# Adding two planes to loaded sums inside the transfer: the dense stage of a convolution-attention hybrid with mixture of experts

## The chip, the cores and the metric

The kernel runs on one core of a Trainium2 chip. The metric is device time in microseconds of one execution. A core has TensorE (PE, matrix products), VectorE (DVE), ScalarE (ACT), GpSimd (POOL) and SyncE (SP); SP, ACT and POOL issue transfers, which sixteen DMA engines carry out. "PEld" in a profile is PE's weight loads. Matrix products go to PSUM, from where VectorE and ScalarE read them.

## What is computed

The input is eight images of 256 channels by 32 x 32, seen as eight items of 1024 tokens with 256 numbers each, all in f32. Cut to what matters:

```python
x = _L0_conv_ref(x, w_qkv, b_qkv, w_out, b_out)   # attention, 8 heads, plus x
t = _to_tokens(x)
t = t + _L1_attn_ref(_ln_t(t), W)                 # attention of tokens on themselves
t = t + _L1_ffn_ref(_ln_t(t), router_w, w1, b1, w2, b2)
x = _from_tokens(t, x)

def _moe(tokens, router_w, w1, b1, w2, b2):       # inside _L1_ffn_ref, 8 experts, top 2
    probs = softmax(tokens @ router_w.T)
    rw, re = top_k(probs, 2);  rw = rw / rw.sum(-1)
    out = tokens
    for e in range(8):
        h = gelu(tokens @ w1[e] + b1[e])
        out = out + combine[:, e:e+1] * (h @ w2[e] + b2[e])
    return out
```

`combine` holds a token's two weights `rw` at its two experts and zero at the other six.

## The kernel before

The items go through the layers one after the other, b = 0 to 7. Items 0 to 6 ("the others") are routed: after their second norm, `dispatch` scatters each token's normed row, twice (once for each of its two experts), into a DRAM tensor of rows sorted by expert. Their running sums (tokens after attention plus the normed tokens) are kept in DRAM as `sums[b]`, 128 partitions x 8 blocks x 256. While item 7 goes through its attention, `experts` works off the 63 blocks of the others' rows, and GpSimd scatters each block's scaled results by an indirect transfer (L1466) into the DRAM tensor `y`. `y` is laid out as two planes: plane k holds, for every token of the others, what its k-th expert gave. `planes[n]` is the view of item n's two planes with the same shape as `sums[n]`. So an other item's final value is `sums[n] + planes[n][0] + planes[n][1]`.

Item 7 itself is not routed. `dense` (L1588) runs all eight experts over all its tokens. Its loop goes over e = 0 to 7 and the two halves n of the tokens, 16 steps. In each step `hidden` makes the first product (`pdh`, L1630, eight PE instructions in the profile) and the gelu on ScalarE (L1639), and `collect` the second product of the step before (`pdy`, L1654, sixteen instructions), which VectorE multiplies by the gate and adds into `t2` (L1664, four instructions of 128 x 256). `pdy` goes to the PSUM pool `ps_acc`, which has two buffers; each holds half of a step's result, so PE can go on with `pdy` only as VectorE's adds free a buffer. `biases` (after the third `hidden`) uses the same two buffers for `pb` (L1618), which VectorE adds into `t2` (L1621).

The class `Results` finishes the others in the shadow of this loop. It has 14 pieces of work, the halves of seven items, each 128 x 1024 f32 = 512 KB. Up to five are in flight. For each one SP loads the half of `sums` into a `total` tile (L1539) and the halves of both planes into a slot (L1541). `collect` calls `others.tick` once a step, after the step's last gated add: `add` puts two VectorE adds of 128 x 1024 behind it (L1551), and `store` transposes the total in 32 x 32 squares (L1573, VectorE) and sends four transfers of 128 KB to the output (L1579); then SP's next loads for that tile are issued. From the step after that on, the gated adds are issued behind the transposition (`others.last`). The last step stores item 7's own second half in two parts, and its transfers alternate between SP and ACT. The transposed tiles `oT` have two buffers.

Each engine's instructions run in the order in which they stand in its queue. Where a transfer has to wait for a landing or for an instruction, its issuing queue waits, and all behind it.

Before the loop, GpSimd's queue ends with the last block's two indirect transfers and four tensor adds (L1120), which put the normed tokens onto item 7's sum.

Of the kernel before, what the change touches and what calls it, by code (L numbers as in the profile page):

```python
# [10 lines left out]
F32 = mybir.dt.float32  # L11
I32 = mybir.dt.int32
AF = mybir.ActivationFunctionType
ALU = mybir.AluOpType
# [5 lines left out]
def kernel(  # L20
# [23 lines left out]
    nc = tc.nc  # L44
    P = 128
    B, C, S = x.shape
    E, D, FF = w1.shape
# [22 lines left out]
    one = ctx.enter_context(tc.tile_pool(name="one", bufs=1))  # L70
    two = ctx.enter_context(tc.tile_pool(name="two", bufs=2))
# [8 lines left out]
    NEXP = 6  # L80
    exp_turn = [0]

    def exp_tile(name, at=None):
        if at is None:
            at = exp_turn[0] % NEXP
            exp_turn[0] += 1
        return expp.tile([P, 1024], F32, tag=f"exps{at}", name=name)
# [148 lines left out]
    NB = NT // NH2  # L236
# [5 lines left out]
    class Split:  # L242

        def __init__(self, first, last):
            self.first, self.last = first, last
# [477 lines left out]
    def attend(b, t1, fill, tick=nothing, n1=None):  # L723
# [28 lines left out]
        for ec in range(NCC):  # L752
            px = big(f"px_{b}_{ec}")
            for dc in range(NCC):
                for n in range(NH2):
                    nc.tensor.matmul(  # L756
                        px[:, ts(n, 512)],
                        WT[:, dc, ts(ec, P)],
                        nT[:, dc, ts(n, 512)],
                        start=(dc == 0),  # L760
                        stop=(dc == NCC - 1),
                    )
            pxs.append(px)
            if ec == 0:
                nc.scalar.copy(a11, px[:, :HALF])
                tick(("xa", ec), nc.vector.tensor_sub(s3_, a11, px[:, HALF:]))
            else:
                nc.scalar.copy(a12, px[:, :HALF])
                nc.scalar.copy(a22, px[:, HALF:])
                nc.vector.tensor_add(s1_, a22, pxs[0][:, HALF:])  # L770
                nc.vector.tensor_sub(s2_, s1_, a11)
                tick(("xa", ec), nc.vector.tensor_sub(s4_, a12, s2_))
# [5 lines left out]
        class Pair:  # L778
# [61 lines left out]
            def rest(self, behind=None):  # L840
# [9 lines left out]
                def even():  # L850
                    tick(("max", 2 * k), self.add(ex0[:, HALF:], self.z, self.low[0], nmax[0]))
                    if k != 1:
                        self.soften()
# [243 lines left out]
    def normed(b, t2, fill, tick=nothing, norm=None):  # L1097

        if norm is None:
            n2 = one.tile([P, NT, DW], F32, tag="n", name=f"n2_{b}")  # L1100
            tokens = n2[:, :, :D]
            tick("normed", layer_norm(t2, tokens, 1e-5, f"f{b}"))
        else:
            n2 = tokens = norm.dst
            written = norm.blocks(NT - 1, NT)
            tick("normed", written)
        fill("norm 2")
        nT = one.tile([P, NCC, S], F32, tag="nT", name=f"n2T_{b}")
        copied = to_channels(tokens, nT, f"n2_{b}")
        tick("turned", copied)  # L1110

        if norm is None:
            nc.gpsimd.tensor_add(t2, t2, tokens)
        else:
            with tc.issue_after(copied.ins):
                fill("turned")
            for part, at in ((n2.first, slice(0, NT - 1)), (n2.last, slice(NT - 1, NT))):
                for cc in range(NCC):
                    some = t2[:, at].rearrange("p i (k cc c) -> p cc i k c", k=NQ, c=SQ)[:, cc]
                    added = nc.gpsimd.tensor_add(  # L1120
                        some, some, part[:, :, ts(cc, P)].rearrange("p i (k c) -> p i k c", c=SQ)
                    )
                    tc.add_manual_dep(added.ins, evicted["scaled"].ins.name, BEHIND)
        fill("normed 2")
        l = logits(b, nT, rT if norm is None else rTs)
        return n2, nT, l
# [191 lines left out]
    def experts(group, behind, table, steps):  # L1318
# [109 lines left out]
        def collect(b, hT, last, squares):  # L1428
            wb, rs = seconds.pop(b), group.size[b] // P
            py = acc(f"pe_{n}_{b}")  # L1430
            at = NCC * FF
            with tc.issue_after(last.ins) if last else nullcontext():
                for r in range(rs):
                    for fc in range(NFC):
                        mm = nc.tensor.matmul(  # L1435
                            py[:, ts(r, D)],
                            hT[:, fc, ts(r, P)],
                            wb[:, ts(fc, D)],
                            start=(fc == 0),
                            stop=(fc == NFC - 1),  # L1440
                        )
            yb = two.tile([P, rs, D], F32, tag="yb", name=f"yb_{n}_{b}")

            def add():
                return nc.vector.tensor_add(
                    yb,
                    py[:, : rs * D].rearrange("p (r d) -> p r d", d=D),
                    b2_flat[:, bass.ds(register(b, 3), D)].unsqueeze(1).to_broadcast([P, rs, D]),
                )

            if squares is not None:
                with tc.issue_after(squares.ins):
                    add()
                    send(b, yb)
            return mm, add, yb
# [45 lines left out]
        def result(b, whole=True):  # L1501
            mm, add, yb = collect(b, hiddens.pop(b), None, None)
            if whole:
                add()
                return send(b, yb)
            return add, lambda: send(b, yb)
# [3 lines left out]
    class Results:  # L1510


        def __init__(self, group):
            self.group = group
            self.todo = [(n, h) for n in range(len(group.items)) for h in range(NH2)]
            wide = one.tile([P, 2, 2, NB, D], F32, tag="v", name="ys_v")
            self.slots = [
                two.tile([P, 2, NB, D], F32, tag="xT", name="ys_0"),
                wide[:, 0],
                two.tile([P, 2, NB, D], F32, tag="xT", name="ys_3"),  # L1520
                wide[:, 1],
                one.tile([P, 2, NB, D], F32, tag="n", name="ys_4"),
            ]
            self.totals = [
                exp_tile(f"total_{i}", i).rearrange("p (i d) -> p i d", d=D)
                for i in range(len(self.slots))
            ]
            self.sent, self.added, self.stored = 0, 0, 0
            self.last = None
            for _ in self.slots:  # L1530
                self.load()

        def load(self):
            if self.sent == len(self.todo):
                return
            n, h = self.todo[self.sent]
            at = self.sent % len(self.slots)
            self.sent += 1
            nc.sync.dma_start(self.totals[at], self.group.sums[n][:, ts(h, NB), :])  # L1539
            for k in range(2):  # L1540
                nc.sync.dma_start(  # L1541
                    self.slots[at][:, k], self.group.planes[n][:, k, ts(h, NB), :]
                )

        def add(self, behind):
            at = self.added % len(self.slots)
            self.added += 1
            total = self.totals[at]
            with tc.issue_after(behind.ins):
                for k in range(2):  # L1550
                    added = nc.vector.tensor_add(total, total, self.slots[at][:, k])  # L1551
            return added

        def store(self, behind):
            at = self.stored % len(self.slots)
            n, h = self.todo[self.stored]
            self.stored += 1
            with tc.issue_after(behind.ins):
                self.last = store(self.group.items[n], self.totals[at], h)
            self.load()  # L1560

        def tick(self, behind):
            if self.added < len(self.todo):
                self.store(self.add(behind))

    def store(b, total, n, parts=1):

# [20 lines left out]
    def dense(b, t2, norm, fill, begin, table):  # L1588
# [59 lines left out]
        def collect(e, n, hT, behind):  # L1648
# [29 lines left out]
            if (e, n) == (E - 1, 0):  # L1678
                with tc.issue_after(added.ins):
                    others.last = store(b, t2[:, ts(n, NB), :], n)  # L1680
# [18 lines left out]
    for b in range(B):  # L1699
        xT = next_x  # L1700
# [7 lines left out]
        if b + 1 < B:  # L1708
            begun = Begin(b + 1, next_x)
            t2 = attend(b, t1, begun.at)  # L1710
            n2, _, l = normed(b, t2, begun.at)
# [85 lines left out]
```

## Time and profile before

| what | us |
|---|---|
| median of three runs (2268.3 to 2272.7) | 2271.99 |
| the profiled execution's own time | 2274.83 |
| its span, first to last instruction | 2273.1 |
| PE busy over the span | 2231.4 (98%) |
| VectorE busy | 1567.1 (69%) |
| GpSimd busy | 309.7 (14%) |
| first product of the dense loop (`pdh`) | starts 2144.28 |
| first pair of plane adds | starts 2158.58 |
| first plane load issued by SP | 2150.06 |
| last transposition | 2267.98, 0.71 long |

How to read it: the profile is one execution, with times counted from the span's start. Its windows give the busy time of each engine in a stretch, with the clock that TensorE was granted (1.00 is full speed) and the mean busy share of the 16 DMA engines; that share can read a little over 1. A timeline row gives start, duration, engine, line, operation, output and inputs and how often it stands there in a row; in brackets is how long the engine sat idle before it and who released it. In the dense loop, a plane load of 512 KB landed a median of 6.4 to 8.1 us after its issue, the load of a total 4.7 us after, a store of 128 KB 3.8 us.

### The profile page before, as it was taken

The numbers are of one execution on the slowest core, as the hardware profiler recorded it, in microseconds if no ns is written. First come the engines' busy times: TensorE is split into PE (matmuls) and PEld (weight loads), VectorE is DVE, ScalarE is ACT, GpSimd is POOL, SyncE is SP. The second block draws the span as 40 slices with busy tenths as digits, with TensorE's granted clock in tenths as the row PEclk, the third lists the DMA queues.
The fourth block names the chain that finished last, engine by engine and source line by source line (L and its number), as shares of the span: only waits on it lengthen the run. The fifth ranks groups of instructions, "written<-read, shape, count | busy, mean of one in ns | idle before, by whom it ended". The sixth has DMA issues, their size and how long they took to land.

```text
span 2273.1 us, 38013 instructions
## 1 busy us (share of the span) xinstructions
PE 2231.4 (98%) x13033; PEld 1200.3 (53%) x13033; DVE 1567.1 (69%) x3924; ACT 1231.3 (54%) x2221; POOL 309.7 (14%) x327
## 2 busy tenths in 40 slices
PE   9999999999999999999999999999999999999998
PEld 3345534563356335543555345534563368885666
DVE  5775678567865787577756775678557857665667
ACT  3664566356636564746554664566355655555411
POOL 1000012000300030002000120002000315551100
PEclk9999999999999999999999999999999999999999
DMA  8996201020102010111011010200032036662485
GB/s 279 357 352 199 53 15 43 3 61 7 51 1 46 19 51 7 31 35 43 15 19 46 20 38 10 55 13 27 1 78 64 31 70 148 149 148 48 120 276 169
DMA packets 273449, 181.89 MB, mean 80 GB/s; under 512 B 191860, under 2 KB 228519, under 8 KB 272232
## 3 DMA queue, kind: packets, MB, share of 16 engines
q1 hardware_dynamic: 260328, 149.16, 24.3%
q0 software_dynamic: 11296, 29.78, 3.6%
q8 instruction: 104, 1.70, 0.3%
q14 instruction: 89, 0.73, 0.1%
q10 hardware_dynamic: 1632, 0.52, 0.1%
HBM read 62.55 MB, written 105.70 MB: 74 GB/s over the span
## 4 chain that ended last, share of the span: by engine, by line
PE 80%; issue 5%; ACT 4%; DVE 4%; SPq 2%; POOL 2%; DMA 1%; POOLq 0%; DVEq 0%; ACTq 0%
PE po L608 20%; PE psc L531 20%; PE pqk L384 7%; PE py L925 7%; PE pr L716 5%; PE pv L414 4%; PE ps L819 3%; PE px L756 2%; POOL y L1466 2%; SPq L908 2%; PE pdh L1630 2%; PE pdy L1654 2%; PE pqk L362 2%; PE ps1z L819 2%; PE ph L1406 1%
## 5 line engine op out<-in xcount | busy, mean ns | idle before, releaser
L572 ACT ACTIVATE ex<-psc,nmax 128x1024 f32<-128x1024 f32 x512 | 570.4, 1115 | 298.8 <-DVE scrap L555 215.6
L608 PE MATMUL po<-ex,vs 64*64 64x512 f32 x4096 | 568.5, 592 | 5.3 <-DVE vs L588 4.3
L531 PE MATMUL psc<-qk,qk 64*64 64x512 f32 x4096 | 566.0, 593 | 3.7 <-ACT ex L572 3.6
L555 DVE TENSOR_SCALAR_CACHE_REDUCE scrap<-psc,nmax 128x512 f32<-128x512 f32 x512 | 384.5, 751 | 158.5 <-PE psc L531 129.8
L546 DVE TENSOR_REDUCE nmax<-psc 128x1 f32<-128x512 f32 x512 | 350.8, 685 | 10.7 <-PE psc L531 10.7
L531 PEld LDWEIGHTS psc<-qk,qk 64*64 64x64 f32 x4096 | 178.0, 132 | 275.1 <-ACT ex L572 129.0
L608 PEld LDWEIGHTS po<-ex,vs 64*64 64x64 f32 x4096 | 172.9, 132 | 284.0 <-DVE vs L588 87.6
L1203 POOL DMA_INDIRECT rows<-n,d_at x112 | 109.2, 975 | 463.4 <-DVE nmax L546 425.1
L384 PE MATMUL pqk<-xT,wqkv 128*128 128x512 f32 x384 | 171.2, 599 | 0.0
L1466 POOL DMA_INDIRECT y<-yb,to x119 | 117.4, 986 | 209.2 <-DVE yb L1459 185.6
L349 ACT ACTIVATE qk<-pqk,b_qks 128x512 f32<-128x512 f32 x124 | 85.6, 690 | 88.8 <-PE pqk L384 79.7
L384 PEld LDWEIGHTS pqk<-xT,wqkv 128*128 128x128 f32 x384 | 71.0, 190 | 99.9 <-issue 77.3
L908 ACT COPY spare<-home 32x256 f32<-32x256 f32 x272 | 109.4, 402 | 17.3 <-DVE home L896 11.9
L414 PE MATMUL pv<-wqkv,xT 128*128 128x512 f32 x244 | 116.4, 600 | 1.0 <-DVE v L436 1.0
L925 PE MATMUL py<-n,spare 128*128 128x256 f32 x512 | 114.9, 379 | 0.0
L1195 POOL IOTA n<- 128x8 f32 x14 | 2.0, 145 | 820.5 <-PE py L925 820.5
L1406 PE MATMUL ph<-xb,w_ring 128*128 128x256 f32 (+1 forms) x488 | 110.7, 370 | 2.9 <-DVE xb L1395 2.8
L716 PE MATMUL pr<-wo,res 128*128 128x256 f32 x512 | 111.9, 379 | 0.7 <-ACT res L627 0.7
L925 PEld LDWEIGHTS py<-n,spare 128*128 128x128 f32 x512 | 96.4, 190 | 20.1 <-issue 4.3
L716 PEld LDWEIGHTS pr<-wo,res 128*128 128x128 f32 x512 | 97.2, 190 | 17.8 <-ACT res L627 4.7
L1418 ACT ACTIVATE hb<-ph,b1T 128x256 f32<-128x256 f32 (+1 forms) x126 | 51.3, 459 | 101.1 <-PE ph L1406 101.1
L1435 PE MATMUL pe<-w_ring,hb 128*128 128x256 f32 x444 | 105.5, 379 | 0.0
(265 smaller groups left out, 2836.8 us busy)
## 6 DMA issues: line engine op xcount, KB each, us to landing
rows<-zero SPq DMA_DIRECT2D x7, 8256.0 KB, 62.4
xr<-rows SPq DMA_DIRECT2D x224, 64.0 KB, 2.0
xs<-in_x_dram SPq DMA_DIRECT2D x64, 128.0 KB, 3.9
ys<-y SPq DMA_DIRECT2D x16, 512.0 KB, 6.4
spare<-home SPq DMA_DIRECT2D x240, 32.0 KB, 1.9
out_dram<-oT SPq DMA_DIRECT2D x58, 128.0 KB, 3.8
xT<-in_x_dram SPq DMA_DIRECT2D x7, 1024.0 KB
sums<-t SPq DMA_DIRECT2D x7, 1024.0 KB
```

The costliest lines, as they stand in the source:

```text
L384: mm = nc.tensor.matmul(pq[:, ts(n, 512)], wqkv[:, cc, t, ts(g, P)], xT[:, cc, ts(n, 512)], start=(cc == 0), stop=(cc == NCC - 1),)
L414: return nc.tensor.matmul(pv, self.xT[:, cc, ts(i, P)], wqkv[:, cc, 2, :], start=(cc == 0), stop=(cc == NCC - 1),)
L531: mm = nc.tensor.matmul(pss[at, h][ts(c, DK), ts(n, 512)], k[r, j * P + c * DK : j * P + (c + 1) * DK], q[r, ts(n, 512)], start=True, stop ...
L546: firsts[at, h] = nc.vector.tensor_reduce(nmax, pss[at, h][:, ts(0, 512)], AX.X, ALU.max, negate=True)
L555: seconds[h] = nc.vector.tensor_scalar(scrap, pss[at, h][:, ts(1, 512)], -1.0, nmaxes[at, h], ALU.mult, ALU.min, accum_out=nmax,)
L572: nc.scalar.activation(ex, pss.pop((at, h)), AF.Exp, bias=nmaxes.pop((at, h)), scale=1.0, accum_out=sums[at][:, h : h + 1],)
L608: mm = nc.tensor.matmul(po[n][ts(h, DK), :], vss[at][keys, h, :], exps[at, h][keys, ts(n, 512)], start=(j == 0 and turn == 0), stop=(j == ...
L716: nc.tensor.matmul(pr[:, :C], res[g][:, ts(i, P)], wo[:, g, :], start=(g == 0), stop=(g == NPAIR - 1))
L908: move(to[ts(k, SQ), a], since[ts(a, SQ), k])
L925: evicted["mixed"] = nc.tensor.matmul(py[:, :D], aT[m], n1[:, m, :], start=(m == 0), stop=(m == NT - 1))
L1406: last = nc.tensor.matmul(ph[:, ts(fc, br)], wb[:, dc * FF + fc * P : dc * FF + (fc + 1) * P], xb[:, dc, :], start=(dc == 0), stop=(dc == ...
L1466: sent = nc.gpsimd.indirect_dma_start(out=group.ways[sum(group.size[:b]) // P + r][:, :], out_offset=bass.IndirectOffsetOnAxis(ap=to[:, r ...
```

## The change

The two planes are no longer loaded into slots of their own. GpSimd issues, for each plane, a transfer that adds what it reads to the `total` tile it writes. The VectorE adds and the slots go; the number of totals in flight is six (`NEXP`) in place of five. SP still loads the totals, and the transposition and the stores stay as they are. In the order in which GpSimd's queue is built, plane 0 of the first three totals comes first, then plane 1 of these three, then the same for the next three; from the seventh total on, plane 0 and plane 1 of a total follow each other. They stand behind the four adds of L1120. The second accumulation into a total waits for the first to have landed, and the first for the load of the sum.

```diff
         def __init__(self, group):
             self.group = group
             self.todo = [(n, h) for n in range(len(group.items)) for h in range(NH2)]
-            wide = one.tile([P, 2, 2, NB, D], F32, tag="v", name="ys_v")
-            self.slots = [
-                two.tile([P, 2, NB, D], F32, tag="xT", name="ys_0"),
-                wide[:, 0],
-                two.tile([P, 2, NB, D], F32, tag="xT", name="ys_3"),
-                wide[:, 1],
-                one.tile([P, 2, NB, D], F32, tag="n", name="ys_4"),
-            ]
             self.totals = [
-                exp_tile(f"total_{i}", i).rearrange("p (i d) -> p i d", d=D)
-                for i in range(len(self.slots))
+                exp_tile(f"total_{i}", i).rearrange("p (i d) -> p i d", d=D) for i in range(NEXP)
             ]
...
         def load(self):
...
-            at = self.sent % len(self.slots)
+            total = self.totals[self.sent % len(self.totals)]
             self.sent += 1
-            nc.sync.dma_start(self.totals[at], self.group.sums[n][:, ts(h, NB), :])
+            nc.sync.dma_start(total, self.group.sums[n][:, ts(h, NB), :])
             for k in range(2):
-                nc.sync.dma_start(
-                    self.slots[at][:, k], self.group.planes[n][:, k, ts(h, NB), :]
-                )
-
-        def add(self, behind):
-            at = self.added % len(self.slots)
-            self.added += 1
-            total = self.totals[at]
-            with tc.issue_after(behind.ins):
-                for k in range(2):
-                    added = nc.vector.tensor_add(total, total, self.slots[at][:, k])
-            return added
+                nc.gpsimd.dma_start(
+                    total, self.group.planes[n][:, k, ts(h, NB), :], accum_op=ALU.add
+                )
...
         def tick(self, behind):
-            if self.added < len(self.todo):
-                self.store(self.add(behind))
+            if self.stored < len(self.todo):
+                self.store(behind)
```

More of the change, by code (lines that the diff above doesn't have):

```diff
@@ L1529, in __init__ @@
             self.last = None
-            for _ in self.slots:
+            for _ in self.totals:
                 self.load()
@@ L1536, in load @@
             n, h = self.todo[self.sent]
-            at = self.sent % len(self.slots)
+            total = self.totals[self.sent % len(self.totals)]
             self.sent += 1
-            nc.sync.dma_start(self.totals[at], self.group.sums[n][:, ts(h, NB), :])
+            nc.sync.dma_start(total, self.group.sums[n][:, ts(h, NB), :])
             for k in range(2):
-                nc.sync.dma_start(
-                    self.slots[at][:, k], self.group.planes[n][:, k, ts(h, NB), :]
-                )
-        def add(self, behind):
-            at = self.added % len(self.slots)
-            self.added += 1
-            total = self.totals[at]
-            with tc.issue_after(behind.ins):
-                for k in range(2):
-                    added = nc.vector.tensor_add(total, total, self.slots[at][:, k])
-            return added
+                nc.gpsimd.dma_start(
+                    total, self.group.planes[n][:, k, ts(h, NB), :], accum_op=ALU.add
+                )
         def store(self, behind):
-            at = self.stored % len(self.slots)
+            at = self.stored % len(self.totals)
             n, h = self.todo[self.stored]
```

## The prediction

> **What bounds the kernel now.** I read the windows of the last 130 us first, then the engines' timelines there, then the chain of waits. The page says PE 98% busy overall, so the question is whether the dense stage (from about 2147 us on) is PE's too, and how much room its other resources have. The windows (busy time of PE, PEld, DVE, ACT, POOL; then granted clock, DMA share, GB/s):
>
> ```profile
> 2156.00:2159.00 3.00, 3.00 (x8) 1.23 (x7) 2.83 (x11) 0.00 (x0) 0.00 (x0) 1.00 1.01 350
> 2159.00:2162.00 3.00, 1.58 (x11) 1.00 (x10) 2.93 (x3) 2.14 (x3) 0.00 (x0) 1.00 1.01 385
> 2165.00:2168.00 3.00, 3.00 (x8) 1.95 (x7) 0.89 (x3) 0.00 (x0) 0.00 (x0) 0.50 1.05 364
> ...
> 2187.00:2194.00 7.00, 7.00 (x26) 4.67 (x25) 5.35 (x7) 1.27 (x2) 0.00 (x0) 1.00 0.91 288
> 2208.00:2215.00 7.00, 7.00 (x26) 4.65 (x25) 5.35 (x7) 1.27 (x2) 0.00 (x0) 1.00 1.00 339
> 2243.00:2250.00 7.00, 7.00 (x26) 4.58 (x25) 5.47 (x8) 1.27 (x2) 0.00 (x0) 1.00 0.32 80
> ```
>
> Two things are to be seen. PE is full in every window of the loop, while VectorE has 1.6 of 7 us free. And the 16 DMA engines are nearly full as well: a share of 0.91 to 1.00 from 2187 to 2229, falling to 0.32 only when the last loads are in and stores alone are left. So the stage is PE's, with the DMA engines second by a few per cent.
>
> VectorE's and GpSimd's timelines show what the change touches (start, duration, engine, line):
>
> ```profile
> 2148.66 4.14 POOL L1120 TENSOR_TENSOR t<-t,n 128x896 f32<-128x896 f32 x2
> 2152.71 0.90 POOL L1120 TENSOR_TENSOR t<-t,n_last 128x128 f32<-128x128 f32 x2
> ```
>
> ```profile
> 2157.00 1.66 DVE L1664 SCALAR_TENSOR_TENSOR t<-pdy,all_gates,t 128x256 f32<-128x256 f32 x4
> 2158.58 2.47 DVE L1551 TENSOR_TENSOR total<-total,ys 128x1024 f32<-128x1024 f32 x2
> 2161.08 1.25 DVE L1573 STREAM_TRANSPOSE oT<-total 128x1024 f32<-128x1024 f32 x1
> 2162.75 0.69 DVE L1621 TENSOR_TENSOR t<-t,pb 128x512 f32<-128x512 f32 x1 [0.42 <-PE pb L1618]
> ...
> 2257.43 2.47 DVE L1551 TENSOR_TENSOR total<-total,ys_v 128x1024 f32<-128x1024 f32 x2
> 2259.94 1.25 DVE L1573 STREAM_TRANSPOSE oT<-total 128x1024 f32<-128x1024 f32 x1
> ```
>
> The adds never wait for data: VectorE runs from the gated adds straight into them. The transposition of a finished half stands in VectorE's queue ahead of the bias adds and the next gated adds, so a late total holds those up, and behind them PE, whose pb and pdy products share two PSUM buffers. PE around the bias products:
>
> ```profile
> 2159.13 1.04 PE L1612 MATMUL pg<-ident,all_gates 128*8 128x128 f32 x8
> 2161.58 6.18 PE L1618 MATMUL pb<-b_rows,gT 8*128 8x256 f32 x16 [1.42 <-ACT gT L1614]
> 2167.70 6.27 PE L1654 MATMUL pdy<-table,dh 128*128 128x256 f32 x16
> ```
>
> **Removed.** 28 adds of 1.22 us (2.47 per tick of the loop) leave VectorE. They are hidden under PE: a tick is 6.89 us (one step of the loop over experts and halves: its gated adds start at 2187.78, 2194.66, 2201.55), of which VectorE uses about 5.4. In the loop this gains nothing. At the end, the last add finishes at 2259.9, but the final products only reach VectorE after 2265; there VectorE is behind PE by some 0.2 to 0.4 us (the transposition of the first own half, 1.25 us, ends at 2265.7 against products due near 2265.2), and that is not the adds' doing. Gain: 0 to 0.4 us; I take 0. The chain of waits does run through the last adds, but rejoins at 2266.03, where the gated add was at work from 2265.61 anyway. The five slots of planes go; a sixth total is loaded ahead, which costs one 512 KB load earlier, in a stretch where DMA is light.
>
> **Moved.** 28 plane loads of 512 KB go from SP's queue to GpSimd's. SP took 0.43 us for one; its queue then holds only stores and the totals' reloads, and nothing there gets later. On GpSimd the nearest row is the direct load L146 (0.92 us) and the indirect L1466 (0.98); 28 x 0.95 = 27 us in a stretch of 105 where GpSimd is idle. But GpSimd is in order: the first accumulation stands behind L1120, which ends at 2153.6, where SP issued its first plane at 2150.06. And plane 1 of a total waits for plane 0 of the same total to land; by the built order the first two groups of three totals go plane 0, 0, 0, then 1, 1, 1, and from the seventh total on each goes 0, 1, with the wait between. Nothing else stands behind them on GpSimd.
>
> **Added: an add within the transfer.** No row of before shows an accumulating transfer. The price of a plain 512 KB: with stores alone a tick takes 0.32 x 6.89 = 2.2 us of the engines; the six windows from 2187 to 2229 average 0.955, or 6.58 us, for four stores and three loads; so one load is (6.58 - 2.2) / 3 = 1.46 us. An accumulation reads the planes' 512 KB and the total's 512 KB and writes 512 KB. Lower bound: the second read is free, 1.46. Upper bound: the slowest row per byte is the stores' (2.2 us per 512 KB, in short runs), and twice that is 4.4. I take one more read of the same length, 2 x 1.46 = 2.92, since the rows are the plain load's own 4 KB rows and the engines show no spare share for a second read.
>
> The Trainium skill speaks against the change here: "Collectives: The Full Stack", section "The bandwidth ceiling: the fold count and why AG ≠ RS ≠ AR", says that a transfer that adds runs at about half the rate of a copy because it needs two source reads on one ring. By it the factor is 2 (1.93 as measured there) and the sum below stands; without it the copy's price would hold and the sum would be near nothing. No run here shows it yet.
>
> **The sum at 2.92.** A tick then needs 2.2 + 1.46 + 2 x 2.92 = 9.5 us of the DMA engines against PE's 6.89. From the first accumulation's start (2153.6 + 0.95 = 2154.6) until the last has landed the engines must do 28 x 2.92 = 81.8, the eight totals that were not loaded ahead 8 x 1.46 = 11.7, and the stores of the thirteen ticks before, 13 x 2.2 = 28.6: together 122 us, to 2276.7, plus about 2 us of landing (a lone 128 KB store lands in 2.2 to 3.3), so 2278.7. The last transposition could have started near 2257.5. After it come 1.25 (transposition) + 0.88 (gated adds that free a PSUM buffer) + 3.45 (PE's last sixteen products) + 0.83 + 0.71 + 4.4 (last stores, 2268.7 to 2273.1 now) = 11.5, so the end is 2290.2, against 2273.1: +17. Two terms more. From the seventh total on, the wait between planes leaves the GpSimd queue empty for landing and issue, 2 + 0.95 = 3 us a total, in which stores and reload (3.66 us) can run, though not always just then: 0 to 0.7 us for each of eight, I take 3 in all. And a stalled PE loses its clock: the 1.42 us pause at 2160 is followed by a granted clock of 0.50, in which the 16 products of pb and the 16 of pdy take 6.18 + 6.27 = 12.4 us, where 32 products of pdy take 7.07 at 2259.87: 5.3 lost. One more such spell costs up to 5.3, part of which the DMA engines use to catch up; I take 3. Sum +23.
>
> The skill's "TensorE: Matmul & The Clock Gate", section "Part 1: The HAM clock gate", has the clock halve only after an idle window of about 3.4 us. The row above shows it halved after a 1.42 us pause, so the row decides; by the rule the stalls of one or two us a tick would cost no clock, and the sum would be 3 us less.
>
> The first tick, by itself: total 0 needs plane 0 landed, then plane 1 behind two others in the queue. At 1.46 that is 2162 to 2163, at 2.92 it is 2154.6 + 2.92 + 2 = 2159.5, then plane 1 starts after the three (2163.4), done at 2166.3, landed about 2168. The bias add that frees PE's buffer ends 1.94 after the transposition's start, and PE needs it at about 2164.7: nothing lost at 1.46, about 5 at 2.92. These 5 are inside the +23, for a PE held early meets totals that are then less late.
>
> **How that stands to the runs.** The profiled execution took 2274.83 (span 2273.1), 2.8 over the median of 2271.99. I add the sum to the median: 2295.
>
> **Rivals.** (1) The second read is hidden: accumulating costs the engines what a load costs. For it: SBUF and HBM are different sources. Then a tick stays at 6.6 of 6.89 us, the first total comes at 2162 to 2163, within 0 to 2 us of PE's need, and the time is 2270 to 2276. It decides as long as a transfer takes under about 2.0 us: 2.2 + 1.46 + 2 x 1.6 = 6.9 is break-even for the tick, and six totals of lead carry a little more. This is the case that ends on the other side. (2) The accumulation is dearer than two reads, up to 4.4: 28 x 1.48 = 41 us more than the sum, plus the emptier queue and clock: 2325 to 2350. For it: the planes of one total are strictly serial, and nothing in before shows how well such transfers overlap. Against: their rows are long (4 KB). (3) Only the first tick is late, later totals just keep up (2.0 to 2.4 us each): 5 for the stall, up to 5 for the clock, so 2277 to 2283. (4) The stall at the first tick shifts PE's pause so that the spell at 0.50 falls away: 5.3 less, 2267. Against: the pause before pb comes from ACT's gT, which the change doesn't touch. That the adds are not moved at all can be excluded: the built order has 28 such transfers on GpSimd and no add left.
>
> **Numbers.** Forecast (2283 to 2315) 0.46; dearer (above 2315) 0.21; first tick only 0.10; hidden 0.17; less than before 0.06. A measurement here tells about 0.2% (4.5 us) from no change. Slower 0.46 + 0.21 + 0.10 = 0.77, same 0.17, faster 0.06. The range 2270 to 2345 takes in the hidden case and most of the dearer one; left out are some 0.07 below and 0.09 above. The forecast's own range is 2283 to 2315.
>
> **What would show it.** DMA share at 1.0 through the stage to some 2275; the last transposition waiting for a transfer and not for VectorE; PE pauses released by VectorE's gated adds; GpSimd idle between two planes of a total. A first transposition at 2168 or later confirms the doubled price, one at 2163 refutes it. If the median time between two totals' landings is under 6.9 us, I am wrong and rival 1 is right.

## The result, and the profile after

| | us |
|---|---|
| changed kernel, median of 4 runs (2284.83 to 2293.24) | 2289.53 |
| kernel before, median beside them | 2270.99 |
| ratio, 95% interval | 1.0082 [1.0060, 1.0103] |
| profiled execution of the changed kernel, span (before: 2273.1) | 2288.3 |

The change made the kernel slower, by 0.6 to 1.0%. The prediction had said 2295 us (2283 to 2315).

The first thing to ask of the new trace is what an accumulation costs. The page's list of transfer queues answers it (q1 holds SP's and ACT's transfers, q0 GpSimd's; packets, MB, share of sixteen engines' span). First the kernel before:

```profile
q1 hardware_dynamic: 260328, 149.16, 24.3%
q0 software_dynamic: 11296, 29.78, 3.6%
```

The same list after the change:

```profile
q1 hardware_dynamic: 256296, 134.47, 22.4%
q0 software_dynamic: 15328, 44.46, 7.0%
```

28 accumulations came to q0: 7.0% of 2288.3 us less 3.6% of 2273.1 us, 160.2 less 81.8, is 78.4 us, or 2.80 us for one. The shares are printed to 0.1%, which leaves this uncertain by some 0.06 us; what else is on q0 hardly varies (81.0 to 81.8 us in e4, e6 and e7, where nothing was added to it).

28 plane loads left q1. There the whole page is a coarse base: e4, with the loads and stores of the kernel before, reads 25.1% of 2269.8 us, 17 us more than the 552.4 of before. So I take the same list for the stretch from 2150 us to the end alone. Before, q1:

```profile
q1 hardware_dynamic: 22192, 27.27, 70.4%
```

After the change, q1:

```profile
q1 hardware_dynamic: 18016, 12.06, 31.9%
```

That is 70.4% of 123.1 us less 31.9% of 138.3 us, 86.7 less 44.1: 42.5 us for the 28 planes and one load of a sum (nine stand there before, eight after), or 1.47 us for a plain load of 512 KB. The bytes are the same; the engines' time nearly doubled.

The windows of the changed kernel show what that does (busy time of PE, PEld, DVE, ACT, POOL, then granted clock, DMA share, GB/s):

```profile
2160.00:2170.00 10.00, 6.61 (x25) 4.50 (x23) 3.10 (x4) 2.14 (x3) 4.32 (x5) 0.79 1.06 210
2170.00:2180.00 10.00, 10.00 (x25) 6.64 (x25) 3.59 (x6) 0.00 (x0) 2.56 (x3) 0.70 1.04 207
...
2210.00:2220.00 10.00, 10.00 (x35) 6.47 (x35) 5.17 (x10) 1.27 (x2) 1.73 (x2) 1.00 1.07 270
...
2240.00:2250.00 10.00, 9.56 (x32) 5.69 (x31) 3.87 (x9) 2.03 (x4) 1.73 (x2) 1.00 0.89 167
2250.00:2260.00 10.00, 7.92 (x30) 5.17 (x29) 3.00 (x6) 1.77 (x3) 2.44 (x4) 1.00 0.88 174
2260.00:2270.00 10.00, 8.42 (x32) 5.62 (x31) 2.79 (x5) 1.26 (x2) 1.87 (x3) 1.00 0.94 184
```

A share of 1.06 at 210 GB/s stands where the kernel before moved 350 to 385 GB/s at 1.01. The engines are full or nearly so from 2160 to 2230 (0.95 to 1.07 in every window), and near 2250, where before only stores were left at a share of 0.32, they are still at 0.9. But from 2230 on they are not quite full, although work is waiting. And PE, which before was full from 2162 to the end of the loop, now loses up to two us of ten.

VectorE's timeline of the changed kernel, its transpositions of the totals (start, duration, engine, line; in brackets the idle time before and its releaser):

```profile
2164.75 1.25 DVE L1555 STREAM_TRANSPOSE oT<-total 128x1024 f32<-128x1024 f32 x1 [6.89 <-DMA total<-y]
2177.67 1.23 DVE L1555 STREAM_TRANSPOSE oT<-total 128x1024 f32<-128x1024 f32 x1
...
2256.63 1.25 DVE L1555 STREAM_TRANSPOSE oT<-total 128x1024 f32<-128x1024 f32 x1 [6.41 <-issue]
2265.33 1.25 DVE L1555 STREAM_TRANSPOSE oT<-total 128x1024 f32<-128x1024 f32 x1 [5.92 <-issue]
2274.46 1.25 DVE L1555 STREAM_TRANSPOSE oT<-total 128x1024 f32<-128x1024 f32 x1 [6.34 <-issue]
2277.28 1.25 DVE L1555 STREAM_TRANSPOSE oT<-t 128x1024 f32<-128x1024 f32 x1
```

VectorE waits 6.89 us for the first total, 2.6 us at most for each of the next eight, and some 6 us for each of the last five, which come at steps of 9 us instead of PE's 6.89. The releaser there reads "issue", since the profile shows no semaphore event for it; what lands at those times are the accumulations, as GpSimd's timeline shows:

```profile
2150.91 2.78 POOL L1532 DMA_DIRECT2D total<-y  x3
...
2190.93 0.85 POOL L1532 DMA_DIRECT2D total<-y  x1 [11.52 <-DMA total<-sums]
2198.33 1.73 POOL L1532 DMA_DIRECT2D total<-y  x2 [6.54 <-DMA total<-y]
2210.00 1.73 POOL L1532 DMA_DIRECT2D total<-y  x2 [9.95 <-DMA out_dram<-oT]
...
2259.29 1.73 POOL L1532 DMA_DIRECT2D total<-y  x2 [6.51 <-DMA total<-y]
2268.44 0.85 POOL L1532 DMA_DIRECT2D total<-y  x1 [7.42 <-DMA total<-y]
```

For the last eight totals GpSimd issues the second plane of one total and the first plane of the next together, and then sits until that first plane has landed: a pair every 8 to 12 us, 10.0 on average from 2198.33 to 2268.44. The 11.52 us at 2190.93 are a wait for SP's reload of a total, which SP issued at 2169.21 and which landed 21.2 us later (median before: 4.7).

PE's timeline of the changed kernel, the rows that follow a pause:

```profile
2162.67 1.99 PE L1600 MATMUL pb<-b_rows,gT 8*128 8x256 f32 x8 [1.42 <-ACT gT L1596]
2166.63 3.78 PE L1600 MATMUL pb<-b_rows,gT 8*128 8x256 f32 x8 [1.97 <-DVE t L1603]
...
2258.78 3.69 PE L1636 MATMUL pdy<-table,dh 128*128 128x256 f32 x16 [2.08 <-DVE t L1646]
2267.48 3.69 PE L1636 MATMUL pdy<-table,dh 128*128 128x256 f32 x16 [1.58 <-DVE t L1646]
2276.61 6.26 PE L1636 MATMUL pdy<-table,dh 128*128 128x256 f32 x16 [5.44 <-DVE t L1646]
```

The chain is to be read from the bottom up: the last total is complete at 2274.4; its transposition stands on VectorE ahead of the gated adds; these free PE's buffer 5.44 us late, and PE's last sixteen products then take 6.26 us (3.62 for sixteen in the loop before), at a granted clock of 0.59 from 2276.6 to 2283.

### The profile page after: what moved, and what is told of

Its sections match the earlier page's. It is cut to its first block, busy times and chain, and to the rows that moved or that the text cites. A ratio compares the mean times of both kernels' runs of the same rounds, so it can differ in the third digit from the quotient of the medians.

```text
span 2288.3 us, 38038 instructions
## 1 busy us (share of the span) xinstructions
PE 2234.7 (98%) x13033; PEld 1200.0 (52%) x13033; DVE 1532.2 (67%) x3896; ACT 1231.2 (54%) x2221; POOL 333.8 (15%) x355
```

## The experiments

Three theories were on the table. A: the doubled price of the transfers fills the DMA engines, and their work sets when the last totals are ready. B: the waits on GpSimd's in-order queue, of a second plane for the first one's landing, set it. C: only the first, late tick and its clock cost time. "Chain" in the expectations is B. Each ratio below is to the kernel before, run beside it.

| run | median us | ratio, 95% interval |
|---|---|---|
| changed kernel | 2289.53 | 1.0082 [1.0060, 1.0103] |
| e1 plain copies for accumulations | 2273.87 | 1.0010 [1.0000, 1.0021] |
| e2 one plane only | 2273.43 | 1.0006 [0.9996, 1.0016] |
| e3 totals taken a step later | 2287.95 | 1.0084 [1.0058, 1.0111] |
| e4 before without VectorE's adds | 2274.11 | 1.0005 [0.9993, 1.0017] |
| e5 14 totals loaded ahead, planes paired | 2275.51 | 1.0015 [1.0004, 1.0026] |
| e6 before, planes loaded twice | 2315.55 | 1.0190 [1.0175, 1.0206] |
| e7 before, bias products cut up | 2270.87 | 0.9991 [0.9982, 1.0001] |
| e8 changed, bias products cut up | 2292.02 | 1.0093 [1.0077, 1.0108] |
| e9 as e5, planes one behind the other | 2296.84 | 1.0105 [1.0079, 1.0131] |
| e10 six totals, planes paired | 2283.09 | 1.0054 [1.0034, 1.0073] |
| e11 as e5, bias products cut up | 2280.65 | 1.0034 [1.0019, 1.0048] |
| e12 six totals, second planes later | 2287.34 | 1.0079 [1.0064, 1.0093] |

**e1: the same transfers on the same queue, without adding.**

```diff
-                    total, self.group.planes[n][:, k, ts(h, NB), :], accum_op=ALU.add
+                    total, self.group.planes[n][:, k, ts(h, NB), :]
```

> The changed kernel with plain transfers in place of the accumulating ones, on the same queue, in the same order and with the same waits between them (the planes overwrite the totals, so the sums are left out of the output). Theory A, the price of the add on the DMA engines: a plain 512 KB costs 1.4 to 1.5 us of the engines instead of 2.8, a step of the loop needs 6.6 of PE's 6.89 us again, and the time falls back to the kernel before, 2270 to 2276. Theory B, the chain on GpSimd's queue (plane 1 waits until plane 0 has landed, and the next total behind it): the waits stay, each round of two landings still takes 8 us or more, and the time stays at 2283 or above.

0.1% is left of the 0.8. VectorE's transpositions in e1 keep PE's tick to the end:

```profile
2245.39 1.23 DVE L1555 STREAM_TRANSPOSE oT<-total 128x1024 f32<-128x1024 f32 x1
2252.27 1.24 DVE L1555 STREAM_TRANSPOSE oT<-total 128x1024 f32<-128x1024 f32 x1
2259.16 1.24 DVE L1555 STREAM_TRANSPOSE oT<-total 128x1024 f32<-128x1024 f32 x1
```

GpSimd still waited 5 to 8 us for landings between its pairs, and it cost nothing. So neither the queue nor its waits cost time at the price of a copy; it takes the accumulation. The page's q0 read 5.7% of 2275.5 us: 129.7 less 81.8 is 47.9, or 1.71 us for a copy on this queue, so that on one queue the factor is 2.80 / 1.71 = 1.64.

**e2: half the accumulations.**

```diff
-            for k in range(2):
+            for k in range(1):
```

> The changed kernel with plane 0 alone accumulated; plane 1 is left out of the output. Theory A: 14 x 2.8 = 39 us of engine time less, a step needs 2.2 + 1.5 + 2.8 = 6.5 us, below PE's 6.89, so 2270 to 2276. Theory B says the same, as the chain is gone too. If the late first transposition alone were the cause (theory C), most of it would go as well, since total 0 is complete after one landing. So this run only has to show that nothing else in the change costs time; above 2280 all three fall.

Again level with the kernel before. 14 transfers of 2.80 us (39 us) take no more than the 28 loads of 1.47 (41 us) did, and fit where those had fitted.

**e3: the first tick.** Every total is taken one step later than in the changed kernel.

```diff
-            others.tick(added)
+            if (e, n) != (0, 0):
+                others.tick(added)
```

> The changed kernel with every total taken one step of the loop later (15 steps are there for 14 pieces). Theory A: the late totals at the end are set by the DMA engines' work, which is the same, so the last total still lands near the same time; only the pause at the bias products goes. 2284 to 2290, and the first transposition does not hold the bias adds. Theory C, the pause before the bias products and the spell of half clock behind it make the time: 2275 to 2280.

The bias products ran in one piece again (6.27 us), the first total was not waited for, and yet no time was gained. VectorE's timeline of e3 shows the lateness move to the end, where the last total comes at 2271.12 and pushes the rest:

```profile
2253.90 1.25 DVE L1555 STREAM_TRANSPOSE oT<-total 128x1024 f32<-128x1024 f32 x1 [6.04 <-issue]
2262.51 1.25 DVE L1555 STREAM_TRANSPOSE oT<-total 128x1024 f32<-128x1024 f32 x1 [5.83 <-issue]
2271.12 1.25 DVE L1555 STREAM_TRANSPOSE oT<-total 128x1024 f32<-128x1024 f32 x1 [5.83 <-issue]
2272.29 1.20 DVE L1555 STREAM_TRANSPOSE oT<-t 128x1024 f32<-128x1024 f32 x1
```

Theory C falls. That what PE lost at the first tick only let the totals catch up is my reading: the reloads go out a step later in e3 too, so the run doesn't weigh the pause alone.

**e4: what the removed adds were worth.**

```diff
-            with tc.issue_after(behind.ins):
-                for k in range(2):
-                    added = nc.vector.tensor_add(total, total, self.slots[at][:, k])
-            return added
+            return behind
```

> The kernel before with VectorE's 28 adds taken out and nothing put in their place; the planes are still loaded, but left out of the output. My step: the adds are hidden, gain 0 to 0.4 us, so 2270 to 2272, ratio 0.999 to 1.001. Rival: the adds do sit on the path at the end (the chain of waits runs through two of them), then 2 to 3 us less.

Level with the kernel before: the 28 adds were hidden, and their removal could bring nothing. (The ratio is the one expected; the median lies above the 2270 to 2272, as that of the kernel before beside it, 2272.45, does.)

**e5: all fourteen totals loaded ahead, the planes in pairs.** SP loads all sums at 2119 to 2143, no reload is left, and GpSimd issues plane 0 of two totals and then plane 1 of both.

```diff
-            for _ in self.totals:
-                self.load()
+            for (n, h), total in zip(self.todo, self.totals):
+                nc.sync.dma_start(total, self.group.sums[n][:, ts(h, NB), :])
+            for two_of in range(0, len(self.todo), 2):
+                for k in range(2):
+                    for j in (two_of, two_of + 1):
...
```

> The changed kernel with fourteen total tiles, one for each piece, in the memory of the former slots and weights: all sums are loaded ahead, and GpSimd's order is plane 0 of two totals, then plane 1 of the two, so that each wait for a landing has another transfer in flight beside it. Theory A: the engines' work is the same but for loads moved ahead; from the first accumulation on 28 x 2.8 + 28.6 of stores + up to 11 of loads = 107 to 118 us, so the last total is 2 to 8 us earlier than the 122 us of the changed kernel, and the time 2281 to 2288. Theory B: with the chain's waits covered the time falls below 2278.

All 28 accumulations run at their doubled price (q0: 7.1% of 2274.7 us less 81.8, or 2.85 us each), and the time is within 0.3% of the kernel before: my expectation under A was missed, and B's met. The windows of e5:

```profile
2210.00:2220.00 10.00, 10.00 (x37) 6.75 (x36) 3.26 (x6) 2.54 (x4) 3.46 (x4) 1.00 1.07 219
2220.00:2230.00 10.00, 10.00 (x37) 6.73 (x36) 2.40 (x5) 1.27 (x2) 0.85 (x1) 1.00 1.05 219
2230.00:2240.00 10.00, 8.63 (x29) 5.05 (x27) 5.57 (x10) 1.27 (x2) 2.60 (x3) 1.00 1.05 202
2240.00:2250.00 10.00, 10.00 (x38) 6.84 (x37) 2.79 (x5) 2.53 (x4) 1.70 (x2) 1.00 1.06 223
2250.00:2260.00 10.00, 10.00 (x35) 6.38 (x34) 6.82 (x11) 1.27 (x2) 0.00 (x0) 1.00 0.70 172
```

The engines are now full from 2180 to 2250 (1.02 to 1.07 in every window), and then done with the accumulations; from the first to the last issue of an accumulation it is 92.7 us (2151.67 to 2244.39), after the change 117.5 (2150.91 to 2268.44). Two things were changed at once, the reloads and the order. Runs e9, e10 and e12 take them apart.

**e6: full engines without any accumulation.** The kernel before loads every plane a second time, into a tile that nobody reads, from SP.

```diff
                 nc.sync.dma_start(
                     self.slots[at][:, k], self.group.planes[n][:, k, ts(h, NB), :]
                 )
+                for half in range(2):
+                    nc.sync.dma_start(
+                        self.spare[:, ts(half, 2)],
+                        self.group.planes[n][:, k, h * NB + 2 * half : h * NB + 2 * half + 2, :],
+                    )
```

> The kernel before, with every plane loaded a second time by SP into an unused tile (the copy is not used; the output is complete). No accumulating transfer, nothing on GpSimd. A step needs 2.2 + 1.46 x 5 = 9.5 us of the DMA engines, nearly what the changed kernel needs. Theory A: slower by 14 to 30 us, 2285 to 2300, with PE held up in the second half of the loop. Theory B or C: these loads touch neither GpSimd's queue nor the first transposition's data, so 2270 to 2276.

Slower, and by more than expected. VectorE's timeline of e6 says why the size was off:

```profile
2212.87 1.25 DVE L1579 STREAM_TRANSPOSE oT<-total 128x1024 f32<-128x1024 f32 x1 [6.84 <-DMA out_dram<-oT]
...
2223.81 1.25 DVE L1579 STREAM_TRANSPOSE oT<-total 128x1024 f32<-128x1024 f32 x1 [5.76 <-DMA out_dram<-oT]
...
2235.12 1.25 DVE L1579 STREAM_TRANSPOSE oT<-total 128x1024 f32<-128x1024 f32 x1 [6.13 <-DMA out_dram<-oT]
```

The transposition waits for a store to free its `oT` buffer, because on SP's queue the stores stand between more loads. That is a wait of its own, at 0.8 to 0.96 of the engines, so the run shows that late transfers stop VectorE and PE, and nothing of the price of an accumulation.

**e7 and e8: PE's half clock at the bias products.** In both, the gates are turned at their old place and the bias products issued one batch later, in pieces between other products; e7 is the kernel before, e8 the changed one.

```diff
             if at == 2:
-                biases()
+                turned_gates = biases()
             if pending is not None:
                 collected = collect(*pending, mm)
+            if at == 2:
+                add_biases(turned_gates)
```

> The kernel before, with the bias step cut in two: the gates' transposition and ScalarE's copy stay where they are, the bias products come one batch of sixteen products later, so that PE has work during the copy. Theory: the 1.42 us pause at 2160 goes, and with it the spell at half clock behind it (5.3 us): 5 to 7 us less, 2264 to 2266. Rival: the clock falls for another reason (the pauses before 2150, or the bias products with 8 rows): only the pause goes, 1 to 1.5 us less, 2269.5 to 2270.5.

> The changed kernel with the same cut. Theory A: the end is set by the DMA engines' work, so that a PE that is earlier by 2 to 7 us waits that much longer for the totals: 2286 to 2291, as without the cut, apart from the time that the clock takes at the very end. Theory C: 5 to 8 us less, 2282 to 2285.

In e7 the granted clock is 1.00 in every window in which PE works, so the spell at half clock is gone; but the gain is 0.1%, less than the theory had, and its interval holds no change. In e8 there is no gain. So the spell at the first tick was not what the change cost.

**e9: the order alone taken back from e5.** Fourteen totals loaded ahead, the two planes of each issued directly one behind the other.

```diff
-            for two_of in range(0, len(self.todo), 2):
-                for k in range(2):
-                    for j in (two_of, two_of + 1):
+            for j, (n, h) in enumerate(self.todo):
+                for k in range(2):
```

> Fourteen totals, all sums loaded ahead by SP, but GpSimd issues plane 0 and plane 1 of a total one directly behind the other, as the changed kernel does; only the pairing of run e5 is taken back. Theory A (what e5 gained is that the eight reloads and the stores of the first ticks left the stretch, and that SP's reloads no longer hold GpSimd up): the last total is ready about as in e5, near 2259 us, and the time is 2274 to 2279 us, no more than 0.2% above e5. Theory B (what e5 gained is that the second plane of a total no longer waits on GpSimd's queue for the first): with 14 waits for the first plane to land back in the queue, about 1 to 2 us each by the 40 us between a DMA share of 1.05 in e5 and 0.92 after the change, the last total is ready near 2272 us and the time is 2283 to 2291 us.

The expectation calls this the changed kernel's order; that holds for the changed kernel's last eight totals alone (its first six go three and three). Theory B was met in direction and exceeded: 2296.84 us, 21 us above e5, with the same transfers. GpSimd's timeline of e9:

```profile
2249.47 1.74 POOL L1534 DMA_DIRECT2D totals_v<-y  x2 [7.38 <-DMA totals_v<-y]
2258.93 1.73 POOL L1534 DMA_DIRECT2D totals_v<-y  x2 [7.72 <-DMA totals_v<-y]
2268.66 1.73 POOL L1534 DMA_DIRECT2D totals_v<-y  x2 [8.00 <-DMA totals_v<-y]
2277.44 0.85 POOL L1534 DMA_DIRECT2D totals_v<-y  x1 [7.05 <-DMA totals_v<-y]
```

One pair is in flight, the queue waits, the next pair goes: 126.8 us from the first to the last issue, 9.1 us a total, though two accumulations and a tick's stores are 2 x 2.80 + 2.2 = 7.8 us of the engines. The mean share over the windows from 2200 to 2280 is 0.88. So with this order the queue sets the pace, and with e5's the engines do. Theory A, as I had put it for this run, falls.

**e10: the changed kernel's six totals and reloads, with e5's pairs.**

```diff
-            for k in range(2):
-                nc.gpsimd.dma_start(
+            if self.sent % 2 == 0:
+                self.add_two()
...
+            for k in range(2):
+                for j in (self.sent - 2, self.sent - 1):
```

> Six totals as in the changed kernel, reloaded by SP after their stores, but GpSimd issues the accumulations of two totals together: plane 0 of both, then plane 1 of both. Theory A: the reloads and the stores stay in the stretch and the pairing takes a reload's total one tick later into GpSimd's queue, so 2284 to 2295 us, the last total near 2272 to 2280 us. Theory B (the chain of the two planes on GpSimd's queue is what costs): the queue is full again as in e5, DMA share above 1.0 from 2160 to 2250 us, and the time is below 2280 us.

2283.09, between the two expectations. The engines were full as B had it (windows of e10):

```profile
2220.00:2230.00 10.00, 10.00 (x40) 7.29 (x40) 2.95 (x6) 1.93 (x4) 1.55 (x2) 1.00 1.06 256
2230.00:2240.00 10.00, 7.34 (x26) 4.61 (x25) 2.79 (x5) 1.27 (x2) 2.58 (x3) 1.00 1.07 268
2240.00:2250.00 10.00, 10.00 (x32) 5.70 (x30) 4.58 (x8) 1.27 (x2) 1.71 (x2) 1.00 1.07 229
```

and the issues took 100.3 us, 17 less than after the change; against e5 it is 7.6 us more, for eight reloads that are 8 x 1.47 = 11.8 us of the engines. But the median is only 6.4 us below the changed kernel, with intervals that overlap. VectorE's waits before its transpositions are now for stores (`out_dram<-oT`, up to 8.4 us), and PE still pauses.

**e12: the same six totals, each second plane behind the first planes of the next two totals.**

```diff
+            self.add(0, self.sent - 1)
+            if self.sent > 2:
+                self.add(1, self.sent - 1 - 2)
```

> The changed kernel with its six totals, its reloads and all 28 accumulations; only the order on GpSimd's queue is another: the second plane of a total is issued after the first planes of the next two totals, so that it finds its first plane landed. Theory B (the cost after the change is that the second plane waits on GpSimd's queue for the first one's landing, which leaves the DMA engines part idle in the last eight totals): the first to the last issue takes about 100 us as in run e10 instead of 117.5, no total is late at the end, and the time is 2276 to 2284 us, 5 to 12 us below the changed kernel. Theory A (the engines' time for the doubled transfers sets the end whatever the order): 2286 to 2294 us as after the change.

The trace did what B asked: 104.0 us from the first to the last issue, and no total late at the end. The time did not: 2287.34, as under A. PE's timeline of e12:

```profile
2222.72 3.69 PE L1647 MATMUL pdy<-table,dh 128*128 128x256 f32 x16 [1.18 <-DVE t L1657]
...
2253.22 3.69 PE L1647 MATMUL pdy<-table,dh 128*128 128x256 f32 x16 [1.10 <-DVE t L1657]
2263.10 5.38 PE L1647 MATMUL pdy<-table,dh 128*128 128x256 f32 x16 [2.75 <-DVE t L1657]
```

The loss moved from the last ticks into the middle: behind the one at the first tick (2.92 us) come five pauses behind VectorE, 6.2 us together, and VectorE waited mostly for stores (up to 8.4 us). A part of this is the run's own: a second plane now stands behind the first plane of a total that SP has still to reload, and GpSimd waited 11 to 16 us four times for that.

**e11: e5 with the bias products cut up.** Both edits are shown above; this was the try at a version that beats both kernels.

> Run e5 (fourteen totals, sums loaded ahead, planes in pairs) with the bias products of run e7 (one batch of gates later, in pieces between other products). If what is left of e5 against the kernel before is TensorE's pause at the bias products of about 4 us with the half clock behind it, the time is 2268 to 2272 us, 2 to 5 us below e5 and level with the kernel before or faster. If the time is set by the accumulations that are still under way when TensorE is done, it stays within 1.5 us of e5.

A miss: 2280.65, above e5 and not below. Cutting the products up helped in none of the three kernels by an amount that can be told from nothing; that e11 lies 5 us above e5, with intervals that overlap, no run here explains. No version with accumulations was faster than the kernel before.

## Why the prediction came out right

- **Removed adds: 0 to 0.4 us, taken as 0.** Right: e4 is level. VectorE's busy time fell from 1567.1 to 1532.2 us, and nothing came of it.
- **Price of an accumulation: 2 x 1.46 = 2.92 us.** Right to 4%: 2.80, and 1.47 for the load. Rival 1 (second read hidden) and rival 2 (up to 4.4) are both refuted by it. The Trainium skill, "Collectives: The Full Stack", section "The bandwidth ceiling: the fold count and why AG ≠ RS ≠ AR", measured AllGather, a collective that copies, at 1.93 times the rate of ReduceScatter, one that adds. Here the factor is 1.90 against SP's loads, and 1.64 against copies on GpSimd's own queue (e1).
- **GpSimd's issue: 0.95 us each.** 0.85; nothing hung on it, as said.
- **First tick.** The marks were 2168 for the doubled price and 2163 against it; the first transposition came at 2164.75, between them. The time alone decides nothing, since in this execution GpSimd came to its first accumulation 2.7 us earlier than I had it (2150.91, not 2153.6). Counted from there I had 14.4 us at 2.92 and about 9 at 1.46; it took 13.8, which speaks for the doubled price. PE's stall there was mis-sized: 5 us foretold, 1.97 seen as a pause and 1.6 in all (the bias products take 7.74 us from first to last, 6.18 before). As said, it is no term of the sum: e3 took it away and gained nothing. Rival 3 falls with it.
- **Engine work to the last total: 122 us.** With the landing and the wait between planes I had 127 us until the last total is there (122 + 2 + 3); it took 122.5, from 2151.9 to 2274.4. But not for the reason given: the sum supposed engines that are full all along at a share of 1. They read above 1 in five of the seven windows from 2160 to 2230, and 0.88 to 0.94 in the four after that, which against 1.06 leaves some 6 us unused. With the measured prices the work alone is 78.4 + 11.8 + 28.6 = 118.8 us at a share of 1, or 112 at 1.06. What the engines did beyond the sum and the time that they stood partly idle nearly cancel, which the prediction did not foresee: that it came so near here is in part luck. Its own sign against it did not appear: the transpositions of the totals follow one another at a median of 8.9 us, not under 6.9.
- **The wait between planes on GpSimd: 3 us in all.** This is the step that was mis-sized. I had counted it as what the queue stands empty beside the engines' sum. Where planes go strictly one behind the other it is the pace itself, 9.1 us a total against 7.8 of engine work, and over fourteen totals it cost 21 us (e9 against e5). In the changed kernel only the last eight totals go so. There it is worth between 2 us (e12) and 6 us (e10) by the medians, with intervals that overlap that of the changed kernel; which of the two, the runs leave open, since each of the new orders brings waits of its own.
- **The reloads: 11.7 us of the sum.** Supported: the issues of e10 take 7.6 us longer than those of e5, and the time is 7.6 us longer too; the two runs differ in the reloads and in where the totals lie.
- **Clock: +3 us.** 2.6 (6.26 against 3.62) in the last products. The row I drew it from was over-read, though; see below. Rival 4 (the spell at 0.50 falls away, 2267) did not happen; e7 shows what it would be worth, about 1 us by the medians, with an interval that holds nothing.
- **The sum: +23.** +18.5, interval 13.6 to 23.4. Of the 4.5 too many, 28 x 0.12 = 3.4 are the price.

So the whole was right because the doubled price is what everything else hangs on: without it the order and the reloads cost nothing (e1), and half of the accumulations cost nothing either (e2). But the price is not enough by itself, as the sum had it: e5 pays it in full, without the reloads and with another order, and loses 0.04 to 0.26%. In the changed kernel two limits, the engines and GpSimd's queue, lie so close together that easing the queue (e10, e12) handed most of the time on to waits for stores.

## What to carry to other kernels

Moving an add from an engine into a transfer can pay only where the engine's time is on the path and the DMA engines have the room (no run here shows such a case): here the adds were hidden, and each transfer went from 1.47 to 2.80 us in a stage whose engines were already 95% busy. Count the DMA engines' work for one step of the loop against the step of the bounding engine, before and after. If accumulations must be, load their targets ahead, and where the engines are near full don't issue two to the same target back to back on an in-order queue: e9 and e5 differ in that alone, and by 21 us. With plain copies (e1) the same waits cost nothing.

## What the runs showed of the hardware that was not expected

- A plain transfer costs GpSimd 0.53 us to issue (e1), an accumulating one 0.85.
- Beside a steady run of accumulations SP's own transfers were slow: one reload landed after 21.2 us instead of 4.7, and SP's issue of four stores stretched from about 2 us to 5.06 (7.69 in e10).
- PE's clock does not follow one length of pause. In e9 pauses of 2.33 and 2.60 us were followed by sixteen products in 5.38 us, one of 2.35 by the usual 3.69; 2.66 in e10 and 2.08 after the change were followed by 3.69 too (the granted clock was 0.69 in the products behind the 2.33, 1.00 in those behind the 2.35). Nor is the 1.42 us pause at the bias products, from which the prediction took its half clock, enough by itself: all sixteen behind it took 6.18 us before, but 4.08 in e9, at a granted clock of 0.95; and in the changed kernel the first eight took 1.99 us at 1.00, and only the eight behind the next pause, of 1.97 us, ran at 0.50. In e7 the same eight-row products, in pieces and without the 1.42 us pause, ran at 1.00 throughout. What decides the moment no run here shows. PE's timeline of e9:

```profile
2162.20 4.08 PE L1603 MATMUL pb<-b_rows,gT 8*128 8x256 f32 x16 [1.42 <-ACT gT L1599]
...
2219.55 5.38 PE L1639 MATMUL pdy<-table,dh 128*128 128x256 f32 x16 [2.33 <-DVE t L1649]
...
2258.41 3.69 PE L1639 MATMUL pdy<-table,dh 128*128 128x256 f32 x16 [2.35 <-DVE t L1649]
```

The Trainium skill, "TensorE: Matmul & The Clock Gate", section "Part 1: The HAM clock gate", has the clock halve after an idle window of about 3.4 us; the pauses of 2.33 and 2.60 us here are shorter and cost clock all the same.
